# Where the corner sums of the first batch's deformable convolution run: VectorE or GpSimd

## The chip, the cores and the metric

The kernel runs on one core of a Trainium2 chip. A core has a matrix engine (TensorE, in the profile PE for the matmuls and PEld for its weight loads), three engines for elementwise work (VectorE = DVE, ScalarE = ACT, GpSimd = POOL), and a queue that starts transfers (SP). The engines run side by side; each works through its own list of instructions in order and waits on semaphores for the others. Metric: device microseconds (us) of one launch, lower is better.

## The reference, cut to what matters

Two images of 256 channels and 64 x 64 pixels go through four layers, all in float32.

```
x = attention(x)               # layer 0: group norm, 4 heads over 4096 pixels, softmax, projection
x = x + position_term          # layer 1
h = relu(bn1(conv1x1(x)))      # layer 2: 256 -> 64 channels
off = conv3x3(h) + boff        #   per pixel and tap (9): an offset (y, x) and a mask
samp[k] = mask * bilinear(h, y_k, x_k)      # four corners with four weights, added up
h = relu(bn2(sum_k w2_k @ samp[k]))
x = relu(bn3(conv1x1(h)) + x)  #   64 -> 256 channels
x = x + two rounds of (group norm, relu, deformable 3x3 conv over 256 channels)   # layer 3
```

What the change concerns is the bilinear sample of layer 2: for every pixel and tap, four rows of 64 channels are fetched, each is multiplied by its weight, and the four products are added.

## The kernel before, in words

**Two stages.** `attention` does layer 0 for both images and, as background work, layers 1 and 2 of image 0 and the first part of layer 2 of image 1. `deform` does the rest. The order of the instructions on TensorE, ScalarE, VectorE and GpSimd is written out by hand in both (`manual_schedule`): an engine gets its instructions in the order in which the Python code issues them. No planner moves them.

**The attention loop.** There are four units: (image 0, heads 0 and 1), (image 0, heads 2 and 3), (image 1, heads 0 and 1), (image 1, heads 2 and 3). A unit has 16 blocks of 256 queries, and a block has 16 steps `n` (4 groups of keys, 2 halves of the queries, 2 heads). A step is: `scores` (two matmuls, L533, into a PSUM tile of 1024 columns; VectorE takes the row maximum, `low`, L542), `exponentials` (ScalarE, L549, needs `low`), `turn` (16 transposes on TensorE, L561, need the exponentials and a free PSUM buffer `tt`), `keep` (copies of the transposes into `et`, on VectorE, L576, or ScalarE, L578), and `attend` (16 matmuls for two steps, L588). Scores are issued two and three steps ahead of the transposes.

**What a block does at its end.** The product with the values is copied to `o` (VectorE, L428). Then `combine` runs on GpSimd: `o` times the softmax shares `f` (L474), the two sums of its four parts (L475, L480), and for every second block of heads 0 and 1 the addition of the position term (L482). `f` comes by DMA through `share_d`. The projection (L498) uses the result `avs` seven steps later.

**The background.** In the units of image 1 the loop calls `background(1)` up to three times for two steps; each call lets one generator go on to its next `yield`. In unit 2, and on into unit 3, that is `conv(0)`, layer 2 of image 0. It goes through 8 blocks of 512 pixels, and each has five groups of taps. A group is four steps (two for the last one), so there are 18 steps in a block and 144 in all. A step handles 128 pixels and two taps (or 256 pixels and one):

- `gather(n + 4)` on GpSimd: two indirect DMAs (L766) into a tile `bfour` of 128 x 512, from a pool of five. It needs the tile that step `n - 1` has done with.
- `weigh(n)` on VectorE (L947): the tile times its weights `bw4`, in place.
- a `yield`, that is, one background call later:
- `add(n, ...)`: two additions on VectorE, 256 columns in place (L956) and 128 columns into `bsmp` (L957; pool of eight).
- when a group's steps are through: four transposes of `bsmp` on TensorE (L967), which are issued one step later behind the next `add` (for the last group of a block one background call behind its own), their copy on ScalarE (L969), and at the end of a block the matmuls of `second` (L976) and `third` (L985), with bn3, the residual and statistics on VectorE (L989 to L993).

In unit 3 `before(1)` comes first in the background: it computes offsets and corner weights of image 1 (`corners`, L671 to L711, many small VectorE instructions). After `conv(0)` the same generator goes on with `early_image`.

`conv(1)`, the same code for image 1, runs in `deform` beside layer 3 and gives VectorE and GpSimd other neighbours.

Of the kernel before, what the change touches and what calls it, by code (L numbers as in the profile page):

```python
# [38 lines left out]
class Net:  # L39
# [734 lines left out]
    class Bottleneck:  # L774
# [148 lines left out]
        def conv(self, b, pools, ps):  # L923
            net, nc = self.net, self.net.nc
# [16 lines left out]
            def weigh(n):  # L941

                i, g, js = steps[n]
                four, ks = fours.pop(n), self.GROUPS[g]
                w = self.w4[b, i]
                w = w[:, js[0], ks[0] : ks[0] + 2, :] if g < 4 else w[:, js[0] : js[0] + 2, ks[0], :]
                nc.vector.tensor_tensor(  # L947
                    four, four, w.unsqueeze(3).to_broadcast([P, 2, 4, CM]), ALU.mult
                )
                return four  # L950

            def add(n, four, sampled):

                i, g, js = steps[n]
                sm = pools["s"].tile([P, 2, CM], F32, name="bsmp")
                nc.vector.tensor_add(four[:, :, 0:2, :], four[:, :, 0:2, :], four[:, :, 2:4, :])  # L956
                nc.vector.tensor_add(sm, four[:, :, 0, :], four[:, :, 1, :])  # L957
                if g < 4:
                    sampled.append(sm.rearrange("p n f -> p (n f)"))
                else:  # L960
                    sampled.extend(sm[:, m, :] for m in range(2))
# [41 lines left out]
            for n, (i, g, js) in enumerate(steps):  # L1003
# [3 lines left out]
                four = weigh(n)  # L1007
                yield "b"
                add(n, four, sampled)
                if last:  # L1010
                    last.popleft()()
# [463 lines left out]
```

## Time and profile before

| | us |
|---|---|
| median of 3 runs (5586.36 to 5594.37) | 5586.81 |
| the profiled execution, its own time | 5402.33 |
| its span, first to last instruction | 5400.6 |
| unit 0 of the attention (first L533 at 58.2) | 694.7 |
| unit 1 (from 752.9) | 732.7 |
| unit 2 (from 1485.6): `conv(0)` in the background | 822.0 |
| unit 3 (from 2307.6): `conv(0)` to 2720, then `early_image` | 816.2 |
| `deform` (from 3123.8) | 2276.8 |

Busy over the span: PE 92%, DVE 79%, ACT 54%, POOL 38%. The units' bounds are the starts of the first L533 matmul of each.

How to read the views: the table by stretches gives for each engine the busy time (and instructions) within a stretch and the clock that TensorE was granted, as a part of full speed. A list of waits says which instruction of an engine waited for which of another. A list of groups says how often an instruction ran, its busy time, its mean, and the idle time before it with what ended that. A timeline lists single instructions: start, duration, engine, line, operation, output and input, and in square brackets the idle time before it.

### The profile page before, as it was taken

Reading aid. Unit: us, or ns where it says so; the run is one execution under the profiler, and the core shown is the slowest. Engines: PE = TensorE matmul, PEld = TensorE weight load, DVE = VectorE, ACT = ScalarE, POOL = GpSimd, SP = SyncE. Lnnn points to the kernel's source line nnn. Section 1 sums busy time; section 2 is a strip of 40 time slices with the busy share of each in tenths; the row PEclk is TensorE's granted clock in tenths of the full one; section 3 lists DMA queues with packets and bytes.
Section 4 is the critical chain, followed back from the end, with each engine's and each line's share of the span. In section 5 each row is a group of like instructions: output and inputs, shape, how many; then the busy total and the mean of one; then the engine's idle time right before and its main releaser. Section 6 shows DMA issues by size and latency. Waiting matters only on the chain.

```text
span 5400.6 us, 97530 instructions
## 1 busy us (share of the span) xinstructions
PE 4976.3 (92%) x37208; PEld 2665.3 (49%) x37208; DVE 4249.0 (79%) x8066; ACT 2897.7 (54%) x5333; POOL 2068.6 (38%) x1946
## 2 busy tenths in 40 slices
PE   8999999999999999999999977767899999999998
PEld 5555555555555555555555533333444444444443
DVE  6877767787668888677766648787899999999998
ACT  5676656666566666566666622222444444444444
POOL 0111101000024343233200047777566566656665
PEclk9999999999999999999999978888999999999999
DMA  5221111101113222222141146666999999999998
GB/s 168 62 89 58 41 64 39 48 29 44 48 54 89 77 82 90 80 78 74 50 136 34 35 156 231 225 223 231 353 333 330 341 360 358 352 390 353 342 349 320
DMA packets 347363, 920.29 MB, mean 170 GB/s; under 512 B 58972, under 2 KB 98698, under 8 KB 346894
## 3 DMA queue, kind: packets, MB, share of 16 engines
q0 software_dynamic: 193536, 679.59, 35.4%
q1 hardware_dynamic: 153358, 234.46, 13.5%
q8 instruction: 292, 4.78, 0.4%
q14 instruction: 177, 1.45, 0.1%
HBM read 815.90 MB, written 89.60 MB: 168 GB/s over the span
## 4 chain that ended last, share of the span: by engine, by line
PE 65%; DVE 17%; issue 6%; DMA 5%; ACT 5%; POOL 2%; SPq 0%; ACTq 0%; DVEq 0%; POOLq 0%
PE sc L533 14%; PE av L588 14%; PE out L1276 10%; PE tt L561 9%; DVE smp L1245 8%; PE pd L726 5%; DMA four<-img,didx 3%; PE pt L1257 3%; DVE low L542 2%; ACT e L549 2%; PE pm L976 1%; POOL bfour L766 1%; DVE bfour L947 1%; PE pm L498 1%; PE pm L247 1%
## 5 line engine op out<-in xcount | busy, mean ns | idle before, releaser
L1245 DVE SCALAR_TENSOR_TENSOR smp<-four,dw,smp 128x256 f32<-128x256 f32 x3456 | 1611.8, 483 | 168.5 <-ACT smp L1239 85.5
L549 ACT ACTIVATE e<-sc,low 128x1024 f32<-128x1024 f32 x1024 | 1147.5, 1121 | 646.0 <-DVE low L542 645.0
L542 DVE TENSOR_REDUCE low<-sc 128x1 f32<-128x1024 f32 x1024 | 1209.5, 1219 | 295.9 <-PE sc L533 288.2
L766 POOL DMA_INDIRECT four<-img,didx x1152 | 1161.5, 1008 | 656.8 <-DVE smp L1245 307.7
L1276 PE MATMUL out<-st,wc 128*128 128x512 f32 x2304 | 1236.8, 619 | 139.7 <-ACT st L1266 111.3
L533 PE MATMUL sc<-k,qs 64*128 64x512 f32 x2048 | 1029.0, 621 | 7.4 <-ACT e L549 7.1
L533 PE MATMUL sc<-k,q 64*128 64x512 f32 x2048 | 1018.7, 620 | 0.0
L588 PE MATMUL av<-et,v 128*64 128x256 f32 x8192 | 999.1, 386 | 0.0
L561 PEld LDWEIGHTS tt<-ident,e 64*128 64x128 f32 x16384 | 647.9, 140 | 559.1 <-issue 245.0
L474 POOL TENSOR_TENSOR o<-o,f 128x1024 f32<-128x1024 f32 x64 | 153.4, 2396 | 1967.1 <-DVE o L428 1182.8
L766 POOL DMA_INDIRECT bfour<-img,bidx x576 | 579.8, 1007 | 665.6 <-DVE bsmp L957 487.3
L561 PE MATMUL tt<-ident,e 64*128 64x64 f32 x16384 | 751.2, 228 | 86.5 <-ACT et L578 69.4
L578 ACT COPY et<-tt 128x512 f32<-128x512 f32 x1280 | 722.2, 587 | 83.7 <-PE tt L561 80.6
L1239 ACT ACTIVATE smp<-four,dw 128x256 f32<-128x256 f32 x1152 | 524.2, 503 | 430.6 <-DMA four<-img,didx 368.9
L576 DVE COPY et<-tt 128x512 f32<-128x512 f32 x768 | 524.6, 683 | 247.3 <-PE tt L561 245.8
L1257 PEld LDWEIGHTS pt<-ident,smp 128*128 128x128 f32 x2304 | 321.1, 144 | 740.7 <-issue 439.1
L1266 ACT COPY st<-pt 128x1024 f32<-128x1024 f32 x288 | 291.0, 1010 | 721.2 <-PE pt L1257 721.2
L588 PEld LDWEIGHTS av<-et,v 128*64 128x64 f32 x8192 | 544.8, 137 | 257.0 <-issue 1.3
L1276 PEld LDWEIGHTS out<-st,wc 128*128 128x128 f32 x2304 | 393.3, 197 | 402.2 <-issue 207.1
L1257 PE MATMUL pt<-ident,smp 128*128 128x128 f32 x2304 | 457.7, 281 | 67.0 <-DVE smp L1245 61.7
L726 PE MATMUL pd<-x,wf 128*126 128x512 f32 (+2 forms) x896 | 460.8, 601 | 8.4 <-DVE wf L1131 7.3
L533 PEld LDWEIGHTS sc<-k,qs 64*128 64x128 f32 x2048 | 351.2, 192 | 229.7 <-issue 123.6
(153 smaller groups left out, 3369.1 us busy)
## 6 DMA issues: line engine op xcount, KB each, us to landing
f<-share_d SPq DMA_DIRECT2D x128, 256.0 KB, 3.9
xb<-xn SPq DMA_DIRECT2D x55, 512.0 KB, 4.0
img<-imgt SPq DMA_DIRECT2D x96, 256.0 KB, 7.0
four<-img,didx POOLq DMA_INDIRECT x1152, 6.1
xa<-res SPq DMA_DIRECT2D x32, 512.0 KB, 2.7
xb<-in_x SPq DMA_DIRECT2D x20, 512.0 KB, 5.4
bfour<-img,bidx POOLq DMA_INDIRECT x576, 3.0
qs<-q SPq DMA_DIRECT2D x64, 128.0 KB, 4.0
```

The lines of the kernel that those rows point to most:

```text
L533: nc.tensor.matmul(s[:, j, :], lhsT=q[u, i // 2][int(h != j)][halves[j], at : at + P], rhs=k[u][c][halves[j], h, :], start=True, stop=True,)
L542: nc.vector.tensor_reduce(low, s, AX.X, ALU.max, negate=True)
L549: nc.scalar.activation(e.rearrange("p j n -> p (j n)"), s, AF.Exp, bias=blk.low[:, g, c : c + 1], accum_out=blk.sum[:, g, c : c + 1],)
L561: nc.tensor.transpose(pt[:, m, :], e[half, m // 4, m % 4 * P : m % 4 * P + P], self.ident[half, half],)
L576: nc.vector.tensor_copy(dst, pt)
L578: nc.scalar.copy(dst, pt)
L588: nc.tensor.matmul(now["av"][halves[h], :], lhsT=v[u][c][:, m, halves[h]], rhs=ets[j][:, m, h, :], start=(m == 0), stop=(m == 7),)
L726: nc.tensor.matmul(pd[:m, r0 * W : r1 * W], lhsT=wt(s, t), rhs=src[:, (y + r0) * W : (y + r1) * W], start=(n == 0), stop=(n == len(srcs) * ...
L766: self.nc.gpsimd.indirect_dma_start(out=dst, out_offset=None, in_=img, in_offset=bass.IndirectOffsetOnAxis(ap=idx, axis=0),)
L1245: nc.vector.scalar_tensor_tensor(smps[s], four[:, c], weight(s, c), smps[s], ALU.mult, ALU.add)
L1257: nc.tensor.transpose(pts[u][:, c, j * P : (j + 1) * P], smp[:, c * P : c * P + P], self.ident,)
L1276: nc.tensor.matmul(outs[ob], lhsT=wc[k][:, c, ob * P : ob * P + P], rhs=sts[u][:, c, :], start=(k == 0 and c == 0), stop=(k == K2 - 1 and ...
```

## The change

In `add`, image 0 (`b == 0`) takes GpSimd for the two additions and image 1 takes VectorE as before. Everything else is as it was; the multiplication in `weigh` stays on VectorE for both images. The order in which the code issues the instructions is the same, so on every engine the others keep their order. Lines from L955 on are one higher after the change.

```
             def add(n, four, sampled):

                 i, g, js = steps[n]
+                engine = (nc.gpsimd, nc.vector)[b]
                 sm = pools["s"].tile([P, 2, CM], F32, name="bsmp")
-                nc.vector.tensor_add(four[:, :, 0:2, :], four[:, :, 0:2, :], four[:, :, 2:4, :])
-                nc.vector.tensor_add(sm, four[:, :, 0, :], four[:, :, 1, :])
+                engine.tensor_add(four[:, :, 0:2, :], four[:, :, 0:2, :], four[:, :, 2:4, :])
+                engine.tensor_add(sm, four[:, :, 0, :], four[:, :, 1, :])
                 if g < 4:
                     sampled.append(sm.rearrange("p n f -> p (n f)"))
                 else:
```

On GpSimd's list the two additions of step `n` come behind the two gathers of step `n + 4` and ahead of those of step `n + 5`, with a `combine` in between where one is issued there.

More of the change, by code (lines that the diff above doesn't have):

```diff
@@ L954, in add @@
                 i, g, js = steps[n]
+                engine = (nc.gpsimd, nc.vector)[b]
                 sm = pools["s"].tile([P, 2, CM], F32, name="bsmp")
-                nc.vector.tensor_add(four[:, :, 0:2, :], four[:, :, 0:2, :], four[:, :, 2:4, :])
-                nc.vector.tensor_add(sm, four[:, :, 0, :], four[:, :, 1, :])
+                engine.tensor_add(four[:, :, 0:2, :], four[:, :, 0:2, :], four[:, :, 2:4, :])
+                engine.tensor_add(sm, four[:, :, 0, :], four[:, :, 1, :])
                 if g < 4:
```

## The prediction

> **What bounds the kernel now.** I read the table by stretches first, one row for each unit of the attention, because the change acts only between 1560 and 2720 us, where `conv(0)` runs.
>
> ```profile
> core 0: us, PE busy (x) PEld busy (x) DVE busy (x) ACT busy (x) POOL busy (x), PEclk, DMA share, GB/s
> 58.20:752.90 694.70, 682.45 (x7377) 395.22 (x7377) 527.78 (x724) 447.84 (x822) 81.59 (x52) 1.00 0.21 66
> 752.90:1485.60 732.70, 726.14 (x7588) 417.33 (x7584) 539.64 (x825) 457.89 (x853) 71.99 (x49) 1.00 0.14 44
> 1485.60:2307.60 822.00, 775.75 (x7656) 444.50 (x7654) 620.82 (x946) 524.96 (x976) 291.42 (x259) 0.98 0.26 78
> 2307.60:3123.80 816.20, 763.22 (x7524) 437.00 (x7521) 570.41 (x889) 536.88 (x998) 156.92 (x133) 0.97 0.23 67
> ```
>
> Columns: length, then busy time (and instructions) of PE, PEld, DVE, ACT and POOL, then the granted clock. In units 0 and 1 TensorE is busy 98 and 99% at clock 1.00: it is the bound. In units 2 and 3 it is busy only 775.75 of 822.00 and 763.22 of 816.20 us, and its clock is 0.98 and 0.97. So beside the added matmuls these units lose 46 + 53 = 99 us to an idle TensorE and, if a mean clock of 0.98 costs 2% of its unit and 0.97 costs 3%, 16 + 24 = 40 us to the clock. That is all that any relief of another engine can win here. Next, whom TensorE waits for, from 1486 to 2840:
>
> ```profile
> PE tt L561 <- ACT et L578: 48.5, 30, 3.4
> PE tt L561 <- DVE et L576: 14.9, 32, 1.6
> ```
>
> The columns are total, times and longest. The transposes wait for the copies that empty their PSUM buffer, on ScalarE above all: 30 waits of 1.6 us mean and 3.4 at most, so few and long. In units 0 and 1 together the first of these lines has 8.7 us. What is late in a long one shows in the timeline of one, on VectorE, GpSimd and TensorE:
>
> ```profile
> 1748.62 0.42 DVE L428 COPY o<-av 128x256 f32<-128x256 f32 x1 [1.16 <-PE av L588]
> 1748.96 0.68 DVE L947 TENSOR_TENSOR bfour<-bfour,bw 128x512 f32<-128x512 f32 x1
> 1749.68 2.46 DVE L956 TENSOR_TENSOR bfour<-bfour 128x256 f32<-128x256 f32 x1
> 1752.17 1.25 DVE L957 TENSOR_TENSOR bsmp<-bfour 128x128 f32<-128x128 f32 x1
> 1753.34 2.34 DVE L542 TENSOR_REDUCE low<-sc 128x1 f32<-128x1024 f32 x2
> ```
>
> ```profile
> 1749.18 2.67 POOL L474 TENSOR_TENSOR o<-o,f 128x1024 f32<-128x1024 f32 x1 [3.87 <-DVE o L428]
> 1751.93 1.33 POOL L475 TENSOR_TENSOR o<-o 128x512 f32<-128x512 f32 x1
> 1753.35 0.72 POOL L480 TENSOR_TENSOR avs<-o 128x256 f32<-128x256 f32 x1
> ```
>
> ```profile
> 1756.38 1.12 PE L561 MATMUL tt<-ident,e 64*128 64x64 f32 x16 [3.02 <-ACT et L578]
> ```
>
> VectorE copies `o` (L428), which releases `combine` on GpSimd. The addition L956 takes 2.46 us and ends when L474 ends (1751.85); L957 takes 1.25 us and ends with L475. Only then come the two maxima L542, then the exponentials, ScalarE's copy, and TensorE's transposes, 3.02 us late. The groups of VectorE and of GpSimd in 1486 to 2840 say how often this is so:
>
> ```profile
> L947 DVE TENSOR_TENSOR bfour<-bfour,bw 128x512 f32<-128x512 f32 x144 | 101.8, 707 | 0.3 <-issue 0.3
> L956 DVE TENSOR_TENSOR bfour<-bfour 128x256 f32<-128x256 f32 x144 | 85.9, 597 | 1.5
> L957 DVE TENSOR_TENSOR bsmp<-bfour 128x128 f32<-128x128 f32 x144 | 62.9, 437 | 4.9
> ```
>
> ```profile
> L766 POOL DMA_INDIRECT bfour<-img,bidx x288 | 282.0, 979 | 557.7 <-DVE bsmp L957 482.1 <-issue 50.1 <-DMA f<-share_d 20.8
> ...
> L475 POOL TENSOR_TENSOR o<-o 128x512 f32<-128x512 f32 x26 | 34.4, 1324 | 2.0
> L480 POOL TENSOR_TENSOR avs<-o 128x256 f32<-128x256 f32 x26 | 23.0, 884 | 2.0
> ```
>
> Undisturbed (medians by tile) L956 takes 0.418 and L957 0.292 us; their means are 0.597 and 0.437. The difference, 0.324 us x 144 = 47 us, is VectorE held up by GpSimd. I went through TensorE's timeline from 1486 to 2840: 34 gaps exceed 0.8 us, 62 us together; 18 of them, **32 us**, follow an L956 or L957 stretched beyond 1 us beside `combine`. The others have other causes (the corners' small operations, L992, the wait for `bod`).
>
> **What the Trainium skill says.** *GPSIMD Engine Reference*, section Specifications: GpSimd's SBUF interface is shared with VectorE, with contention for VectorE instructions that have two SBUF inputs or run in a 2-port mode. The trace agrees: L956 and L957 (two SBUF inputs) stretch beside L474 and L475, while the maxima and copies from PSUM keep 1.22 and 0.68 us. Same page, section Performance versus the Vector engine: a two-input addition is about 1.96 times slower on GpSimd. Here, at 256 columns, L480's median 0.728 us stands against 0.418, 1.74 times. *TensorE: Matmul & The Clock Gate*, Part 1: the array's clock halves after an idle window of about 3.4 us. The trace agrees in kind: after the gap above the stretch 1755.7 to 1762.5 ran at 0.50; but a gap of 3.0 us was enough.
>
> **The change part by part.**
>
> (1) *VectorE loses the additions*: 85.9 + 62.9 = 149 us of busy time, 47 of them stalls. On the path lie the 32 us of gaps. Behind these 18 I find, in fine slices of the clock, eleven half-clock stretches of 3.4 us; half of 37.5 us is 19 us of lost matmul time. In the episode above the next to be late would be the scores: TensorE issues them from 1749.05 to 1751.0, so the maxima could start some 3 us earlier and TensorE would be waiting for nothing but itself. Gross gain: 32 + 19 = **51 us**. I count nothing for the rest, as VectorE waits 167 us for scores (L542) in this stretch and is no bound outside such moments.
>
> (2) *GpSimd gains them*: 0.728 us for 256 columns, and from L475 (512: 1.277) and L480 a slope of 2.15 ns a column, so 0.45 us for 128. 1.18 us x 144 = 170 us, into an engine busy 291 of 822 us in unit 2. TensorE's work covers that; were it uncovered it would be the 170. The strided views may cost more than these dense rows: up to 1.5 times, 255 us, still covered.
>
> (3) *The queue on GpSimd.* Its 482 us of waiting for L957 (the row of L766) turns into waiting for L947, at the same pace, since the gathers of step n + 4 still follow the addition of step n - 1. No DMA is added; the gathers land in 3.0 us, three steps (some 24 us) before use. What is new: an addition can stand behind `combine` (2.36 + 1.28 + 0.73 us, with L482 2.36 more) and behind two gathers (2 x 1.25 with their issue), 8 to 10 us after its multiplication, and the transposes L967 on TensorE wait for it. Laying the additions into GpSimd's recorded times, group by group, 8 of the 40 groups of transposes come late, by 0.1 to 3.9 us, **13 us** in all; with half clock after the longest I take 16. Ends: 5 (TensorE is itself late there) and 40 (strided views slow, and each delay lengthened). Behind the waiting transposes stand the next scores, so this is fully on the path. `combine` itself moves by up to 2 us, and `o` is needed again 8 or more us after `combine` starts, so VectorE's L428 does not wait.
>
> (4) *The port.* Now L947 meets `combine` first. One comes each 1160 / 144 = 8 us; falling evenly into three instructions it is held for (2.36² + 1.28² + 0.73²) / 2 / 8 = 0.48 us per `combine`: 26 x 0.48 and 0.35 for each of 8 L482 are 15 us of VectorE. Before, 47 us of stalls made 32 us of gaps; now VectorE has 0.71 us a step in hand, so I take a third, **5 us** (0 to 15). GpSimd's new additions hold it too: 1.18 / 8 of the L947 meet one, for 0.35 us, 144 x 0.15 x 0.35 = 7 us, nearly all hidden: **1 us** (0 to 7).
>
> (5) Units 0 and 1 and `deform` hold none of it: nothing.
>
> Sum: -51 + 16 + 5 + 1 = **-29 us**; 5402.3 becomes 5373. The median of the timed runs is 184 us above the profiled execution, which the page doesn't explain; I take the same difference off it: 5586.8 - 29 = **5558 us**. No change means within 0.2%, 11 us, about what a measurement of this kernel can tell.
>
> **The rivals.**
>
> *The stall only changes its victim* (about the same): L947 is held like the additions were, the gaps shrink by half only (gain 25 us), and the late transposes take 20 back: 5582 us. For it: an L947 took 2.07 us beside L482. Against: its mean is 0.707 in this stretch, near the undisturbed 0.683, so it mostly runs ahead of `combine`, as at 1748.96.
>
> *The queue on GpSimd decides* (slower): each of 26 `combine`s puts the transposes behind it 2.9 us late, 75 us, with half clock (1.7 us) after half of them, 22 us: -51 + 97 = +46, so 5633 us. It decides from 1.5 us a `combine` on with that share of half clock. For it: eight groups come late already by my reckoning. Against: most others have 1 to 9 us in hand, since they are issued one step behind their additions.
>
> *Larger gain*: VectorE's slack also ends the gaps under 0.8 us and TensorE keeps full clock: another 30 us, 5528 us.
>
> *The change doesn't do what it says*: excluded, the written order moves just these instructions.
>
> **How the numbers follow.** Forecast, with the larger gain: 0.68. The stall that changes its victim, or costs at the upper end of (3): 0.17. The queue: 0.15. The likeliest case spans 5527 (larger gain) to 5575. The range 5525 to 5596 adds the middle case and the slower one's near end, leaving out some 0.15 above and 0.04 below.
>
> **What would show it.** Right: no additions of image 0 on VectorE; TensorE idle in units 2 and 3 down from 99 to about 70 us, clock 0.98 to 0.99; a new wait of L968 (the transposes) for the sums on GpSimd of 10 to 20 us; GpSimd's additions 0.73 and 0.45 us; units 0 and 1 and `deform` as they were. Wrong: that wait above 50 us, or L947 at a mean above 0.95 us, or GpSimd's additions twice the price.

## The result, and the profile after

| measurement | before, us (runs) | changed, us (runs) | ratio, 95% interval |
|---|---|---|---|
| the one the forecast is held against (long) | 5593.72 (20) | 5578.24 (20) | 0.9974 [0.9963, 0.9985] |
| e2, another session (quick) | 5407.1 (33) | 5407.72 (13) | 1.0002 [0.9993, 1.001] |
| e8, a third session (long) | 5590.7 (34) | 5573.34 (13) | 0.9972 [0.9962, 0.9982] |

The forecast was 5558 us, that is, a gain of 29 us. The measurement gives 15.5 us, a ratio of 0.9974 against the forecast 0.9948: the sign is right, the size half. A time can be read only beside the runs of before in its own session, because the sessions were of two kinds: in some, called quick here, every run of before takes 5397 to 5415 us, in the others, called long, 5570 us or more. In the quick one the change wins nothing, in the long ones 15 to 17 us. The profile of before that the prediction was made from (5402.33 us) is of the quick kind; the time that the forecast was subtracted from is of the long kind.

The changed kernel's first profile (a long session, 5572.85 us, span 5571.1) by stretches; these are the rows of units 2 and 3, with the columns of the table shown of before:

```profile
1486.20:2307.10 820.90, 769.15 (x7658) 440.78 (x7656) 537.39 (x752) 524.69 (x976) 415.33 (x453) 0.99 0.27 79
2307.10:3133.00 825.90, 768.15 (x7524) 437.18 (x7520) 537.09 (x795) 536.03 (x998) 216.63 (x227) 0.96 0.23 66
```

VectorE's busy time fell from 620.82 to 537.39 us in unit 2, GpSimd's rose from 291.42 to 415.33. TensorE's did not come closer to its unit: 769.15 of 820.90 and 768.15 of 825.90 us, so 52 + 58 = 110 us idle. The profile in the prediction has 99, but is of the other kind; kind by kind it is 100.2 us in e1 (before) and 102.3 in e2 (changed), and 117.3 in e7 (before) and 108.9 in e8 (changed). Its waits between 1486 and 2840 (total, times, longest):

```profile
PE pm L968 <- POOL bsmp L958: 39.7, 18, 3.5
PE tt L561 <- ACT et L578: 20.6, 18, 3.4
PE tt L561 <- DVE et L576: 11.0, 23, 1.6
```

The two lines that before was judged by (L561) fell: their sum is 64.9 us in e1 and 29.1 in e2, 68.3 in e7 and 31.5 in e8, so 36 or 37 us less, a little more than the 32 that step (1) had named as gaps. But a line that before did not have (0.6 us there) stands on top: the transposes wait 39.7 us, in 18 waits, for the sums on GpSimd. The groups of VectorE and GpSimd in the same stretch:

```profile
L947 DVE TENSOR_TENSOR bfour<-bfour,bw 128x512 f32<-128x512 f32 x144 | 117.7, 817 | 0.0
```

```profile
L766 POOL DMA_INDIRECT bfour<-img,bidx x288 | 284.7, 989 | 85.4 <-issue 43.7 <-POOL bsmp L958 35.2 <-PE sc L533 3.0
L957 POOL TENSOR_TENSOR bfour<-bfour 128x256 f32<-128x256 f32 x144 | 112.1, 779 | 308.0 <-DVE bfour L947 277.7 <-PE sc L533 17.5 <-PE pm L968 10.2
L958 POOL TENSOR_TENSOR bsmp<-bfour 128x128 f32<-128x128 f32 x144 | 70.7, 491 | 11.3
```

The additions cost 0.779 and 0.491 us on GpSimd in the mean; the medians, 0.731 and 0.455, are as forecast. L947 rose from 0.707 to 0.817 us. GpSimd's wait before its gathers (482 us for L957) has become 278 us of waiting for L947, less than before by 204: it has more to do and lags behind VectorE more of the time. One of the 18 waits, on GpSimd and on TensorE:

```profile
1766.06 0.74 POOL L957 TENSOR_TENSOR bfour<-bfour 128x256 f32<-128x256 f32 x1
1766.88 0.46 POOL L958 TENSOR_TENSOR bsmp<-bfour 128x128 f32<-128x128 f32 x1
1767.60 1.39 POOL L766 DMA_INDIRECT bfour<-img,bidx  x1 [0.27 <-POOL bsmp L958]
1769.30 0.95 POOL L766 DMA_INDIRECT bfour<-img,bidx  x1 [0.30 <-issue]
1770.27 0.73 POOL L957 TENSOR_TENSOR bfour<-bfour 128x256 f32<-128x256 f32 x1
1771.08 0.46 POOL L958 TENSOR_TENSOR bsmp<-bfour 128x128 f32<-128x128 f32 x1
1771.81 1.40 POOL L766 DMA_INDIRECT bfour<-img,bidx  x1 [0.27 <-POOL bsmp L958]
1773.51 1.21 POOL L766 DMA_INDIRECT bfour<-img,bidx  x1 [0.30 <-issue]
1774.74 0.73 POOL L957 TENSOR_TENSOR bfour<-bfour 128x256 f32<-128x256 f32 x1
1775.55 0.45 POOL L958 TENSOR_TENSOR bsmp<-bfour 128x128 f32<-128x128 f32 x1
```

```profile
1772.52 0.55 PE L968 MATMUL pm<-ident,bsmp 128*128 128x128 f32 x3
1776.05 0.33 PE L968 MATMUL pm<-ident,bsmp 128*128 128x128 f32 x1 [2.98 <-POOL bsmp L958]
```

The last of the four transposes waits 2.98 us for the sum that GpSimd ends at 1776.0. No `combine` runs in this stretch. Each step takes GpSimd two additions and two gathers, and the additions L957 start at 1766.06, 1770.27 and 1774.74: 4.2 and 4.5 us a step. In a busy stretch of the loop VectorE's multiplications L947 come no slower than that (1763.15, 1767.48, 1771.69 in this profile). The last `combine` had ended at 1759.2. So what GpSimd fell behind while it ran it, it does not make up before the transposes of the next groups.

### The profile page after: what moved, and what is told of

The parts are those of the page before. It is cut to its first block, busy times and chain, and to the rows that moved or that the text cites. A ratio compares the mean times of both kernels' runs of the same rounds, so it can differ in the third digit from the quotient of the medians.

```text
span 5571.1 us, 97612 instructions
## 1 busy us (share of the span) xinstructions
PE 4985.8 (89%) x37208; PEld 2664.4 (48%) x37208; DVE 4131.0 (74%) x7778; ACT 2883.6 (52%) x5333; POOL 2245.1 (40%) x2234
## 4 chain that ended last, share of the span: by engine, by line
PE 62%; DVE 14%; issue 8%; POOL 5%; ACT 5%; another core or an unknown queue 5%; DMA 2%; SPq 0%; ACTq 0%; POOLq 0%; DVEq 0%
PE av L588 14%; PE sc L533 13%; PE out L1277 9%; PE tt L561 9%; DVE smp L1246 8%; PE pd L726 5%; PE pt L1258 3%; POOL bfour L766 2%; ACT e L549 2%; PE pm L498 1%; PE pm L247 1%; PE pm L977 1%; DVE low L542 1%; POOL bfour L957 1%
## 5 line engine op out<-in xcount | busy, mean ns | idle before, releaser
L533 PE MATMUL sc<-k,qs 64*128 64x512 f32 x2048 | 1026.2, 619 | 7.2 <-ACT e L549 6.8
L533 PE MATMUL sc<-k,q 64*128 64x512 f32 x2048 | 1014.6, 618 | 0.0
L474 POOL TENSOR_TENSOR o<-o,f 128x1024 f32<-128x1024 f32 x64 | 152.2, 2378 | 1945.7 <-DVE o L428 1200.8
L561 PEld LDWEIGHTS tt<-ident,e 64*128 64x128 f32 x16384 | 646.4, 140 | 528.5 <-issue 256.6
L561 PE MATMUL tt<-ident,e 64*128 64x64 f32 x16384 | 747.5, 228 | 57.7 <-ACT et L578 41.7
L578 ACT COPY et<-tt 128x512 f32<-128x512 f32 x1280 | 721.5, 586 | 96.9 <-PE tt L561 84.8
L576 DVE COPY et<-tt 128x512 f32<-128x512 f32 x768 | 525.0, 684 | 260.8 <-PE tt L561 256.9
L1258 PE MATMUL pt<-ident,smp 128*128 128x128 f32 x2304 | 458.8, 282 | 82.1 <-DVE smp L1246 70.1
L533 PEld LDWEIGHTS sc<-k,qs 64*128 64x128 f32 x2048 | 349.2, 191 | 225.9 <-issue 121.5
```

The source lines that it names most:

```text
L533: nc.tensor.matmul(s[:, j, :], lhsT=q[u, i // 2][int(h != j)][halves[j], at : at + P], rhs=k[u][c][halves[j], h, :], start=True, stop=True,)
L561: nc.tensor.transpose(pt[:, m, :], e[half, m // 4, m % 4 * P : m % 4 * P + P], self.ident[half, half],)
L576: nc.vector.tensor_copy(dst, pt)
L578: nc.scalar.copy(dst, pt)
L1258: nc.tensor.transpose(pts[u][:, c, j * P : (j + 1) * P], smp[:, c * P : c * P + P], self.ident,)
```

## The experiments

All kernels but the controls are the changed kernel or before, with the edit shown. "Attention" is the time from the first L533 of unit 0 to the last one of unit 3, read from each kernel's profile; it repeats within 0.5 us for before in quick sessions (3065.6, 3065.8) and in long ones (3087.7 in e5, 3087.5 in e7) and for the changed kernel in long ones (3074.1, 3074.5), and within 2.1 us for the kernel of e6 and e11, so it is sharper than the total. Of it, 1.7 us are scatter in unit 0, which holds nothing of the change: it takes 694.7 us in most profiles and 696.3 or 696.4 in e4, e6, e12, e13 and e14. Idle times of TensorE are those of units 2 and 3.

### e1 and e7: before, once more, in a quick and in a long session

No edit.

> The kernel before, unchanged, profiled once more and timed against itself. The profile shown of before has a span of 5400.6 us, while the timed runs have a median of 5593.7; the changed kernel's profile has 5571.1. If the 180 us are a matter of the single execution (its second stage), this profile has an attention of 3065.6 us within 1 us and a deform stage of some 2440 to 2470 us instead of 2277, and the ratio of the times lies within 0.2% of 1. If the two profiles' difference in deform were an effect of the change, deform would again take 2277 us.

> The kernel before, unchanged. On the chip of the first experiments: 5407 us, deform 2277 to 2280. On the chip of the first measurement: 5594 us; then its profile shows whether its attention is 3066 us or longer, and how long TensorE stands still in stalls over 8 us between 3150 and 3950 (178 us in the changed kernel's profile there).

Measured: e1 5408.27 us, ratio 1.0001 [0.9993, 1.0010], attention 3065.8, the rest as in the first profile. TensorE's waits in e1:

```profile
PE tt L561 <- ACT et L578: 49.9, 30, 3.4
PE tt L561 <- DVE et L576: 15.0, 32, 1.6
```

The expectation that the 180 us were a matter of the single execution is wrong: all 33 runs of before shared by e1 to e4 took 5400 to 5415 us.

e7: 5589.76 us, ratio 0.9999 [0.9986, 1.0012]; attention 3087.5, so 22 us longer than in the quick session, in units 2 and 3:

```profile
1486.10:2325.90 839.80, 780.65 (x7660) 447.99 (x7656) 621.05 (x946) 526.17 (x977) 291.58 (x259) 0.98 0.26 77
2325.90:3146.30 820.40, 762.23 (x7522) 435.66 (x7519) 570.66 (x889) 537.25 (x998) 157.00 (x133) 0.97 0.23 66
```

The same two waits are 52.6 and 15.7 us in e7. The rest of the 186 us between the two profiles, 164 us, lies in `deform`, where TensorE stands still 11 times for more than 8 us between 3150 and 3950, 185 us together; e1 has no such stop, the other profiles of quick sessions have one to three. Units 0 and 1 are the same to 0.1 us in e1 and e7.

### e2 and e8: the changed kernel, in a quick and in a long session

No edit.

> The changed kernel once more. Both theories: attention 3074 us within 1 us as in the first profile (8.5 us more than before), so the gain of 15 us in the timed runs must come from deform. If the gain lies in deform, deform here is shorter than the control's by some 24 us; if it lies only in the scatter of the timed runs, the ratio moves to 1.000 within its interval.

> The changed kernel, unchanged. On the chip of the first experiments: 5407 us, ratio 1.000. On the chip of the first measurement: 5578 us, ratio 0.997; then the difference to the control's profile lies in deform, if the stalls over 8 us differ, or in the attention, if the control's is longer than 3074 us.

Measured: e2 attention 3066.7 us, 0.9 more than e1; e8 attention 3074.5, 13.0 less than e7. Waits of TensorE in e2:

```profile
PE pm L968 <- POOL bsmp L958: 38.1, 17, 3.4
PE tt L561 <- ACT et L578: 18.8, 13, 3.3
PE tt L561 <- DVE et L576: 10.3, 24, 1.6
```

and its units 2 and 3, to be compared with the rows of before in the prediction (clock 0.98 and 0.97):

```profile
1485.50:2304.00 818.50, 770.58 (x7656) 440.18 (x7654) 534.99 (x752) 523.85 (x976) 414.40 (x453) 0.98 0.27 79
2304.00:3124.90 820.90, 766.52 (x7526) 437.22 (x7521) 535.53 (x795) 536.23 (x998) 215.84 (x227) 0.96 0.23 66
```

Both kernels lose about the same to an idle TensorE in the quick kind of session: 100.2 us in e1, 102.3 in e2. The gain in L561's waits (36 us) and the new wait (38 us) cancel. e2's expectation of 3074 us was the value of a long session. That the gain would lie in `deform`, as it also had it, fell: in the long sessions 13 of the some 16 us lie in the attention, where before has become slower.

### e3: the transposes later, four groups of five

```
-                if last:
-                    last.popleft()()
+                if last and n >= last[0][0]:
+                    last.popleft()[1]()
...
-                last.append(lambda g=g, sm=sampled: sts.append(transpose(g, sm)))
+                last.append((n + 2 - b, lambda g=g, sm=sampled: sts.append(transpose(g, sm))))
```

> The changed kernel, with the transposes of a group of image 0 issued one step later (two steps behind their last addition; the last group of each block as it was). Queue theory (the attention gave back its gain because TensorE waits 39.7 us for the sums on GpSimd): of these, 27 us in the groups concerned go, with some half-clock time, so the attention falls from 3074 to about 3035 to 3045 us, the wait of the transposes to 13 us. Port theory (GpSimd's additions and combine hold VectorE up, and the waits of the transposes only show it): the wait moves to the other transposes, L561, and the attention stays at 3070 or above.

Measured, in a quick session: 5375.23 us, ratio 0.9942 [0.9928, 0.9956], attention 3038.4: 28.3 us below e2. The wait was expected at 13 us and is

```profile
PE pm L968 <- POOL bsmp L958: 17.1, 8, 3.4
```

so 21 us of it are gone. TensorE's idle time fell by 20 us, from 102.3 to 82.1; the other 8 are time at half clock (mean clock of the two units 0.987 and 0.962, where e2 has 0.979 and 0.960). L561's wait for ScalarE is 20.6 us, where e2 has 18.8: the port theory's shift of the wait to these transposes did not happen. The queue theory stands.

### e4: the gathers behind the addition

```
-                gather(n + ahead)
+                if b:
+                    gather(n + ahead)
...
                 add(n, four, sampled)
+                if b == 0:
+                    gather(n + ahead)
```

> The changed kernel, with the two gathers of step n + 4 issued behind the addition of step n instead of ahead of its multiplication (image 0 only). Queue theory: an addition that stands behind combine no longer has two gathers of 1.25 us each in front of it as well, so the longest lags fall from 9 to 7 us and the wait of the transposes from 39.7 to 15 to 25 us; attention 3050 to 3062 us. Port theory: no change beyond 3 us, as the same instructions hold the port for the same time.

Measured: 5407.85 us, ratio 1.0001 [0.9992, 1.0009], attention 3069.6, 2.9 us above e2, of which 1.7 lie in unit 0.

```profile
PE pm L968 <- POOL bsmp L958: 28.9, 14, 3.4
PE tt L561 <- ACT et L578: 25.0, 20, 3.4
```

A miss: the sums' wait fell to 28.9 us only, not to 15 to 25, and L561 waits more (25.0, and 15.8 for VectorE, where e2 had 18.8 and 10.3). What the sums' wait gave, 9 us, L561's waits took back, 12 us. In the same trace the multiplication L947 has a mean of 0.915 us, 0.801 in e2, so VectorE is held up more; that this is what lengthens L561's waits is likely, but no run shows it apart.

### e5: before, with the later transposes

The edit of e3, on before.

> The kernel before (all additions on VectorE), with the transposes of a group of image 0 issued one step later. Queue theory (in the changed kernel the transposes waited for GpSimd's queue; before, TensorE waited 0.6 us for the sums): attention within 4 us of the control's 3065.8, ratio 1.000. Rival, the order theory (it is the later place of the transposes on TensorE that wins, whoever adds): attention falls by some 27 us here too, to about 3040, ratio 0.994.

Measured, in a long session: 5594.91 us, ratio 1.0006 [0.9997, 1.0015]; attention 3087.7, e7 has 3087.5. The order theory fell: moving the transposes wins nothing while VectorE adds (run in a long session only). Written before it was known that before's attention depends on the session, the expectation names the control of the quick one; e7 is the one to compare with.

### e6, e11 and e13: all transposes later

The edit of e3, and for the last group of each block of image 0:

```
+                    for _ in range(0 if b else 2):
+                        yield "any"
                     last.popleft()[1]()
```

> The changed kernel with all transposes of image 0 later: those of groups one to four of a block one step, those of the last group two background calls. Queue theory: the wait of the transposes for the sums falls from 17.1 us (with only the first four groups later) to under 5, the attention from 3038.4 to some 3022 to 3030 us, the ratio to before to 0.991 to 0.993. Order theory: the 16 added background calls only push work from unit 2 to unit 3, attention 3036 to 3042.

> The changed kernel with all transposes of image 0 later, once more. Queue theory: on the chip where the kernel before takes 5407 us a gain of 38 to 55 us (ratio 0.990 to 0.993; the first four groups alone gave 31 us there); on the chip where it takes 5591 us again 0.9866 within its interval. If the 71 us there were scatter between chips' runs, the ratio moves to 0.992 or above.

> The changed kernel with all transposes later, on the same chip as e12. Both theories: attention 3026 to 3031 us, one gap of some 3.6 us behind a row of gathers on a slower chip and none on the faster one; ratio 0.987 to 0.989 on a slower chip, 0.990 to 0.993 on the faster one.

Measured:

| | session: before, us | this, us | ratio, 95% interval | attention, us |
|---|---|---|---|---|
| e13 | quick: 5405.32 | 5356.56 | 0.9911 [0.9899, 0.9924] | 3020.6 |
| e6 | long: 5590.7 | 5519.39 | 0.9866 [0.9848, 0.9884] | 3027.5 |
| e11 | long: 5652.0 | 5580.97 | 0.9891 [0.9874, 0.9908] | 3029.6 |

This kernel beats both others in either kind of session. Three expectations missed: e6's ratio is below the 0.991 to 0.993 named, e13's attention is below the 3026 to 3031 us named, and e11's ratio is not e6's, in a session whose before takes 61 us more. In e6's session 60 of the 71 us won lie in the attention (e7 has 3087.5); why `deform` is shorter too, no run tells. The wait of the transposes in e6 is

```profile
PE pm L968 <- POOL bsmp L958: 4.4, 3, 1.8
```

In the quick kind the attention is 45 us below before's (3065.8) with 4.9 us of that wait left. TensorE's idle time is 71 us, 29 below e1's, and the mean clock of units 2 and 3 0.993 and 0.968 against 0.977 and 0.969, some 14 us. So most of the gross gain of step (1), 51 us, was there to be had.

### e9 and e10: combine on VectorE

```
-                    due(at + 20, self.combine)
+                    due(at + (22 if units[u][0] else 20), self.combine)
...
+                    eng = (nc.gpsimd, nc.vector)[units[self.u][0]]
-                    nc.gpsimd.tensor_mul(o, o, self.f)
+                    eng.tensor_mul(o, o, self.f)
```

and so on for L475, L480 and L482: in the units of image 1 `combine` goes to VectorE and is issued two steps later; in e9 on the changed kernel, in e10 on before. Lines from L474 on are one higher.

> The changed kernel, with combine (L474, L475, L480, L482) of the units of image 1 on VectorE, two steps later in the written order so that f has landed. Queue theory (an addition is late because combine and two gathers stand in front of it): with combine gone from GpSimd the longest lag of an addition falls from 9 to about 4 us and TensorE's wait for the sums from 38 to under 12 us. VectorE has some 2.3 us of combine in a block now, 1.2 us more with L482, ahead of the maxima; if that costs TensorE 1 us in each of 26 blocks, the attention comes out 5 to 20 us below the changed kernel's. Rival (the lag comes from the gathers and from GpSimd's own slowness): the wait stays above 25 us.

> The kernel before, with combine of the units of image 1 on VectorE, two steps later; nothing but the gathers is left on GpSimd there. Port theory of the stalls (L956 and L957 stretch because combine holds the port): their means fall from 597 and 437 to 418 and 292 ns, L947 to 683, the 18 gaps behind stretched additions go (32 us), and the attention changes by -20 to +10 us, as VectorE now does combine itself (26 x 2.3 and 8 x 1.2 us). Rival (the additions are slow for another reason, such as the gathers' descriptors): the means stay above 550 and 400 ns.

Measured, in a long session: e10 5653.83 us, ratio 1.0009 [0.9996, 1.0022], attention 3112.6. The groups of VectorE:

```profile
L957 DVE TENSOR_TENSOR bfour<-bfour 128x256 f32<-128x256 f32 x144 | 60.2, 418 | 1.5
...
L958 DVE TENSOR_TENSOR bsmp<-bfour 128x128 f32<-128x128 f32 x144 | 42.1, 292 | 4.9
```

With no elementwise work on GpSimd beside them, all 144 pairs take 0.418 and 0.292 us in the mean, none over 0.43, and L947 takes 0.682. The gathers still run: 69 of the multiplications and 17 of each addition overlap with one and are no longer than the others by more than 0.01 us. So the stretching of the additions in before came from `combine`, not from the gathers. This agrees with what the Trainium skill says on the shared SBUF interface (*GPSIMD Engine Reference*, Specifications): it is shared with VectorE, with contention for VectorE instructions that have two SBUF inputs.

The total is that of before in the same session: what the additions no longer lose, VectorE's own `combine` takes. The transposes wait 54.5 us for VectorE's copies L577, where e7 has 15.7 (L576), and TensorE is idle for 117 us in both. The attention is 25 us above e7's, beyond the range expected, but e7 is of another session, in which before takes 61 us less; before was not profiled in e10's session, so this comparison stays open.

e9 5657.56 us, ratio 1.0015 [1.0001, 1.0029], attention 3096.7, 22 us longer than e8's, which is of another session; expected were 5 to 20 less. TensorE's first two waits:

```profile
PE tt L562 <- DVE et L577: 66.9, 43, 4.1
PE tt L562 <- ACT et L579: 8.5, 17, 1.0
```

The wait for the sums is not in the list at all: without `combine` in GpSimd's list no transpose waits for it (gathers and additions are as in the changed kernel). Nor is that only because TensorE comes later: in e2 the addition L957 starts up to 10.0 us after the end of its multiplication, and more than 4 us after it in 55 of the 144 steps; in e9 (L958) at most 3.6 us. This settles that `combine` makes GpSimd late. What it costs on VectorE I had put too low: the transposes wait 66.9 us for VectorE's copies, 10.5 in e8.

### e12 and e14: gathers four in a row

The kernel of e6, and

```
-                gather(n + ahead)
+                if b:
+                    gather(n + ahead)
+                elif n % 2:
+                    gather(n + ahead - 1)
+                    gather(n + ahead)
```

In before GpSimd issues four or more gathers back to back (less than 0.4 us between them) 18 times once the steps of `conv(0)` have begun; in the changed kernel never, since two additions stand between each two pairs, and both have one row of eight ahead of the first step. In e7 seven gaps of TensorE above 0.8 us (13.8 us) end within 3 us of the end of such a row, in e8 one (2.5 us), in e1 and e2 none.

> The changed kernel with all transposes of image 0 later, and its gathers issued four in a row at every second step (for steps n + 3 and n + 4) instead of two at each. Theory of the rows (on the slower chips TensorE stands still while four gathers or more go out in a row): on a slower chip gaps of TensorE above 0.8 us behind such a row come up in conv(0), 7 or more with 14 us or more against one with 3.6, and the attention is 10 to 50 us longer than e13's; on the faster chip no such gap. Rival (the gaps come from something else in the order of before, such as the additions on VectorE): at most two such gaps, and a difference to e13 only in the transposes' wait for the sums, since an addition can stand behind four gathers.

> The kernel of e12 once more. On a slower chip, theory of the rows: 7 or more gaps of TensorE above 0.8 us behind a row of four gathers, 14 us or more, attention 3045 to 3080 us against 3027.5 and 3029.6 of the same kernel with gathers two by two; ratio to before above 0.991. Rival: at most two such gaps, attention below 3042 us. On the faster chip both expect none, and an attention of 3032 us as in e12.

Measured: e12, quick, 5366.67 us, ratio 0.9926 [0.9914, 0.9938], attention 3031.8, 11.2 above e13; no gap behind a row. e14, long, 5609.41 us, ratio **1.0028** [1.0017, 1.0038] where e6 has 0.9866; attention 3106.8, some 78 us above e6 and e11; 18 gaps behind a row, 24.8 us, where e6 has one (3.6 us). One of them, on GpSimd, ScalarE and TensorE:

```profile
1693.43 0.96 POOL L766 DMA_INDIRECT bfour<-img,bidx  x1
1694.69 0.95 POOL L766 DMA_INDIRECT bfour<-img,bidx  x1 [0.30 <-issue]
1695.94 0.95 POOL L766 DMA_INDIRECT bfour<-img,bidx  x1 [0.30 <-issue]
1697.19 0.95 POOL L766 DMA_INDIRECT bfour<-img,bidx  x1 [0.30 <-issue]
```

```profile
1695.76 0.21 ACT L549 ACTIVATION_READ_ACCUMULATOR e<-sc,low 128x1 f32 x1
1699.34 1.07 ACT L578 COPY et<-tt 128x512 f32<-128x512 f32 x2 [3.37 <-remote]
```

```profile
1699.98 0.27 PE L561 MATMUL tt<-ident,e 64*128 64x64 f32 x1 [2.27 <-ACT et L578]
```

From the third gather until 1.2 us after the end of the last, ScalarE starts nothing for 3.37 us, with a releaser that the profile does not name, and TensorE loses 2.27 us behind it; VectorE stands still for 4.43 us beside them.

So in the long sessions rows of gathers do hold TensorE up, and the price was put too low (10 to 50 us). But the gaps right behind the rows are only 24.8 of the 78 us. TensorE's idle time is 47 us above e6's (123 against 76; its wait for ScalarE's copies L578 alone rises from 22.7 to 56.0 us), and the lower clock (0.988 and 0.959 against 0.993 and 0.971) makes some 15 more; the remaining time is not accounted for. Of the 11 us in the quick session 4 are the longer wait for the sums (8.7 us against 4.9) and some 5 are half clock. The expectations speak of chips; e12 and e14 have the same chip number on record and fell into different kinds of session, so that number does not tell the kind.

## Why the prediction was wrong, point by point

- **Step (3), the queue on GpSimd, is the step that failed.** It put the late transposes at 13 us and took 16, with ends of 5 and 40. They wait 38.1 us in e2 and 39.7 in the first profile: at the upper end. How late a single addition can be was foreseen (8 to 10 us; 10.0 in e2), but not how many transposes that reaches: in e2 14 of the 40 groups wait, by 0.1 to 5.4 us, not 8 by up to 3.9. I had laid the additions into before's recorded times, and two things speak against that. In those times TensorE still has its own gaps, so it comes to the transposes later than it does once they are gone. And I reckoned with a step in 8 us (three steps as some 24 us), whereas in busy stretches one comes in some 4.2 us, the time that GpSimd itself needs for a step. A lag that `combine` causes is therefore handed on: in most of the 14 groups the late sum is the second to fifth behind the last `combine`. How much of the missing 25 us each of the two makes, no run tells. e9 shows that the lag starts at `combine`; e3 and e13 show the price of it, 28 and in all some 46 us below e2.
- **Step (1), the gross gain, was right** in its gaps, with 36 us in L561's waits (e1 to e2) for 32, and wrong in the rest of the sum: the 19 us of half clock did not come: between 1486 and 2850 TensorE has 33 gaps above 0.8 us in e2, 69 us together, where e1 has 35, 64 us, and the clock is 0.98 and 0.96 where it was 0.98 and 0.97. With the 22 us that (3) falls short of the waits, this term makes up the 29 us forecast and more. Where the new wait is away (e13), 45 us come of the 51.
- **Step (2)**, the price on GpSimd, was right: 0.731 and 0.455 us against 0.728 and 0.45; the strided views cost nothing.
- **Step (4), the port:** L947 rose from 0.707 to 0.801 us in e2, 144 times, which is 14 us of VectorE; forecast were 15 for `combine` and 7 for the additions. How much of it reaches TensorE no run tells apart from the rest.
- **Step (5)** holds for units 0 and 1 (694.7 and 732.6 us). With it the sum of a quick session reads: 36 us of L561's waits are won, 38 us of waits for the sums are new, the half clock is not won, TensorE's idle time goes from 100.2 to 102.3 us, and the attention from 3065.8 to 3066.7.
- **The base was wrong too.** The 184 us between the profile and the timed runs were taken for a constant beside the work. They are the difference between two kinds of session, and 22 us of it lie in units 2 and 3 of before. In the long kind the change has a gain of its own, of 13 us in the attention, most likely by breaking up the rows of gathers: gaps behind them fall from 13.8 us to 2.5 (e7 to e8), and e14, in another kernel, puts the rows back and loses 78 us. So the measured 15.5 us come from an effect that the prediction does not hold, while the one that it holds gave nothing (e2): that the sign was right was luck. The remaining 2 to 4 us, between attention and total, lie within the scatter of `deform`.
- **The signs named in advance:** GpSimd's prices and units 0 and 1 came as said; the idle time, the clock and the wait for the sums did not. Yet none of the three signs of being wrong came either: the wait stayed below 50 us, where 38 was enough to use up the gain.
- **The rivals:** "the queue on GpSimd decides" named the right wait and its right place; its price of 2.9 us a `combine` was too high (39.7 / 26 = 1.5 us), which is the very point from which it said that it would decide. "The stall only changes its victim" was wrong in mechanism: L561's waits fell by more than half and did not come back in e2.

Open is why long sessions exist, and what holds TensorE, ScalarE and VectorE up in them while gathers are issued in a row: the profile names no releaser, and no run here tells. The queue behind `combine` was seen in both kinds, gaps behind the rows of gathers in the long kind only.

## What to carry to other kernels

When an operation moves to an engine with a slower step, compare that engine's time for one step with the spacing of the steps in their densest stretch, not with the mean: a lag that it can't make up there is handed on to the consumers behind it. Then move the consumer in the written order by as much as the lag: here one step for four groups of five and two background calls for the fifth turned a change worth nothing in the quick session into 0.9% there, and 0.3% in the long ones into 1.1 to 1.3%. And lay new work into times from which the expected gain has been taken off already, since the consumer comes earlier by just that gain.

## What was not expected of the hardware

- In the long sessions four indirect gathers in a row come with stops of ScalarE of up to 3.4 us and of VectorE of up to 4.4 us without a named releaser (e14), and a kernel that differs from another only in issuing the gathers in fours instead of twos is 1.4 to 1.6% slower against before (1.0028 against 0.9866 in e6 and 0.9891 in e11); in the quick session 0.15% (0.9926 against 0.9911).
- Two VectorE additions of 128 and 256 columns keep 0.292 and 0.418 us beside GpSimd's gathers (e10) and reach up to 2.98 and 2.47 us beside its elementwise instructions (before).
- The 3.0 us that the prediction found enough for half clock are not the least: in before TensorE ran 3.4 us at half clock behind a gap of 2.29 us (from 1950.3 us on) and behind one of 1.58 us (from 1970.7 us on).
